# A graph-network layer in f32 on one core: Strassen's scheme for batch 0 as well, a first convolution group of 128 columns, and a new table of exchanged places

## The chip, the cores and the metric

The kernel runs on one core of a Trainium2 chip. Its time is the device time of one execution in microseconds; smaller is better. Three timed runs of the kernel before gave 2005.38, 2008.96 and 2012.02 us.

## The reference

For 32 graphs of 512 nodes with 256 features, everything in f32 (`x` is first normalised over its features and cut at 0; `h` is the result):

```python
xc = transpose(h, (0, 2, 1))
x_conv = relu(bn(conv1d(relu(bn(conv1d(xc, conv1_w, 0))), conv2_w, 8)) + xc)   # conv2 has 17 taps
s = h @ w_se.T + b_se                                  # 3 numbers for each node
A = exp(-(|s_n|^2 + |s_m|^2 - 2 s_n.s_m)) * adj        # 512 x 512 for each graph
x_nmp = A @ relu(h @ w_msg.T + b_msg)
gi = concat(x_conv, x_nmp) @ w_ih.T + b_ih             # three gates of 256: r, z, n
gh = h @ w_hh.T + b_hh
r, z = sigmoid(gi_r + gh_r), sigmoid(gi_z + gh_z)
n = tanh(gi_n + r * gh_n)
out = x + (1 - z) * n + z * h
```

## The kernel before

One function, `tile_adj_preln_gnn_kernel`, issues everything by hand. Its work is cut into five streams (`streams`), Python generators that each issue a small piece and then say when the next piece may go.

`rows` makes the first convolution (`conv1`, two 128x128 weights by 512 columns for each half of the output) of the batches that a group needs, and leaves it in `h1`. `begins` prepares the batches that come later: normalised input, transposed, stored to DRAM (`HD`), and read again by the users. `graphs` computes messages, the exponential (`kernel_exp`), the mask product (`masked`, on VectorE) and the gather (`gather`). `conv` is the second convolution, and `gates` the three gates of each batch (`gates(b)`, with one `unit(o)` for each half of the output features).

The second convolution is of Winograd's kind, nested twice. The 32 x 512 positions become 928 columns (29 for each batch, `U`), and these are cut into seven groups by `STARTS`. Each group has 25 products. VectorE prepares their operands (`operands`, `fives`, `ends`: the tiles `x` and `xd`), with weights `w` that are made in the first group and read back from DRAM (`wd`) in the others. A product of the first group is 16 matmuls (8 for one with a zero factor), as wide as the group; in the other groups a third operand makes 12 do. ScalarE takes the results out of PSUM (`n`, `z`), VectorE sums them (`summed`), and `evacuate` hands them to the batches.

The batches of a group are `batches(g)`, which counts those that have any column in it; a batch that straddles two groups is computed in both, with its own part of the columns. With the first boundary at 116 = 4 x 29 columns, the first group has exactly batches 0 to 3, and `G = 4` says so.

A gate batch is computed in a plain form or in Strassen's form, by one line:

```python
fast = FIRST_FAST <= b < B - PLAIN          # FIRST_FAST = 1, PLAIN = 1, B = 32
```

The plain form takes 18 matmuls of 512 columns for each half. The fast one treats the gates r and z as a 2 x 2 block product with seven products, each of 3 matmuls of 256 columns, and 6 of 512 columns for the third gate. It needs sums of the weights (`weight_sums`, once, in `wsum`) and of the data (`data_sums`, for each batch, in `t`). In it a PSUM bank is partly filled by ScalarE before TensorE adds to it:

```python
ps_z = acc.tile([P, N], F32, name="ps_acc")
act.activation(ps_z[:, lo], ps_r[:, lo], AF.Copy)
```

The order in which the streams are served is settled when the program is built. A planner keeps a model of each engine, computes when each stream can go on, and takes among the able streams the one whose clock is furthest behind. `OTHERS` is a table of exceptions: at the numbered choice it takes another one. While nothing is able, `keep_warm` issues dummy transposes of the identity (`ps_acc<-ident`), in the early part only. The batches up to 7 (`TURNED`) are transposed on TensorE, the later ones on VectorE.

Of the kernel before, what the change touches and what calls it, by code (L numbers as in the profile page):

```python
# [31 lines left out]
G = 4  # L32
U = 29
Q = 18

STARTS = (0, 116, 252, 388, 523, 658, 793, 928)
NG = len(STARTS) - 1
UG = max(j - i for i, j in zip(STARTS, STARTS[1:]))
PER = (STARTS[-1] - STARTS[1]) / (NG - 1) / U
TURNED = 8  # L40
# [10 lines left out]
def kernel(  # L51
# [32 lines left out]
    B, N, D = x.shape  # L84
# [4 lines left out]
    def sizes(g):  # L89


        nu = STARTS[g + 1] - STARTS[g]
        return nu, ND * nu, 2 * ND * nu, ND * (nu + 1)
# [98 lines left out]
    def elements(t):  # L192
        n = 1
        for k in t.shape[1:]:
            n *= k
        return n
# [52 lines left out]
    def on_pe(out, ins, took):  # L249
        nonlocal now  # L250
        now = max(now, after("PE", [out], ins)) + took
        note("PE", [out], ins, now + 0.163)

    def matmul(ps, lhsT, rhs, **more):
        nonlocal narrow
        few = lhsT.shape[0] < 32
        on_pe(ps, [lhsT, rhs], (0.2675 if few else max(0.2145, 0.005 + elements(ps) / 600.0)) + 0.1 * (few != narrow))
        narrow = few
        nc.tensor.matmul(ps, lhsT, rhs, **more)  # L259
# [88 lines left out]
    def load_gates(b):  # L348
        if b >= B or b in HB:
            return  # L350
        settle_stores()
        HB[b] = late.tile([P, ND, N], F32, name="hTb", bufs=2)
        sp.dma_start(HB[b], HD[b])
        HB_AT[b] = done(HB[b])
# [21 lines left out]
    def load_sums(b):  # L376
        if b < B and b not in XN:
            settle_stores()
            XN[b] = late.tile([P, ND, N], F32, name="xnb", bufs=2)
            for d in range(ND):  # L380
                sp.dma_start(XN[b][:, d, :], ND_[b, d])
            XN_AT[b] = done(XN[b])
# [17 lines left out]
    ident = const.tile([P, P], F32, name="ident")  # L400
# [27 lines left out]
    def input_of(g):  # L428
        return h1[:, : Q * sizes(g)[3]].rearrange("p (q i v) -> p q i v", q=Q, i=ND)

    def zeros(g):
        at = input_of(g)
        for b in range(B + 1):
            v = U * b - STARTS[g]
            if 0 <= v <= sizes(g)[0]:
# [94 lines left out]
    def conv1(g, b, o):  # L530

        hT = HT[b] if g == 0 else HR[b]
        v0, at = U * b - STARTS[g], input_of(g)
        first, last = max(0, -v0), min(U, sizes(g)[0] - v0)
# [178 lines left out]

    RING = 6
    PLAIN = 1
    FIRST_FAST = 1
    W_BASE, taken = [], 0

    def new_w():
# [178 lines left out]
    def batches(g):  # L898

        return range(STARTS[g] // U, (STARTS[g + 1] - 1) // U + 1)  # L900
# [195 lines left out]
    def weight_sums():  # L1096


        for k, w in enumerate((whh, wih[:, :ND], wih[:, ND:])):
            a11, a12 = w[:, 0, :D], w[:, 1, :D]  # L1100
            a21, a22 = w[:, 0, D : 2 * D], w[:, 1, D : 2 * D]
            s1, s2, s4 = (wsum[:, k, j, :] for j in range(3))
            dve.tensor_tensor(s1, a21, a22, op=ALU.add)
            dve.tensor_tensor(s2, s1, a11, op=ALU.subtract)
            dve.tensor_tensor(s4, a12, s2, op=ALU.subtract)
            dve.tensor_tensor(a21, a11, a21, op=ALU.subtract)

    OPEN, NEW, NEW_DONE, NEW_B, MIXED = 0, [], [], [FIRST_FAST], [0, 0]
    UPDATED, LEFT = [0, 0], [0]
    T_AT, T_STEP = {}, {}  # L1110
    sums_free = [FIRST_FAST, FIRST_FAST]

# [120 lines left out]
    def begin(b):  # L1233

        nonlocal begun, turning
        if b >= TURNED:
            yield lambda: b not in NORMS
            yield NORM_AT[b]  # L1240
            xs = XS.pop(b)
            pool.dma_start(XD_[b].rearrange("(c p) d -> p c d", p=P), xs)
            yield done(XD_[b])
            xb = xs.rearrange("p c d -> p (c d)").rearrange("p (o n) -> p o n", o=ND)
            for o in range(ND):
                blocks(xb[:, o, :], XD_[b].rearrange("(k i) d -> i k d", i=32), o)
            yield max(done(xb), front.free("hT", 2))
            settle_stores()
            HT[b] = front.tile([P, ND, N], F32, name="hT", bufs=2)
            turning = True  # L1250
            for o in range(ND):
                dve.transpose(HT[b][:, o, :], xb[:, o, :])
                if o < ND - 1:
                    yield dve.free
            yield dve.free + 0.4
            pool.dma_start(HD[b], HT[b])
            begun, turning = b + 1, False
            if b + 1 < B:
                later(now + 0.3, lambda: load(b + 1))
            return  # L1260
        if b == 2:
            yield lambda: told > 0
        yield lambda: b not in NORMS
        yield NORM_AT[b]
        turning = True
        for d in range(ND):
            yield gps.free("ps_g")
            norm_t(b, d)
            if d == ND - 1:
                begun, turning = b + 1, False  # L1270
                if b < 2 or G <= b < TURNED - 1:
                    load(b + (G if b < 2 else 2))
            yield now

    def rows(g, b):
        nonlocal made, made_at
        for o in range(ND):
            yield gps.free("ps_g")
            conv1(g, b, o)
            if o == ND - 1 and b == batches(g)[-1]:  # L1280
                made, made_at = g + 1, act.free + LAG
            yield now
        HT.pop(b, None)
# [43 lines left out]
    def gates(b):  # L1327
# [11 lines left out]
        hT = HB[b]  # L1339
# [77 lines left out]

        fast = FIRST_FAST <= b < B - PLAIN
        if b == B - PLAIN:
# [24 lines left out]
        def unit(o):  # L1444
# [55 lines left out]
            if fast:  # L1500
                if o == 0:
                    if b == FIRST_FAST:
                        weight_sums()
# [10 lines left out]
                def term(ps, weight, data, begin=False, end=False, of=(0, 1, 2)):  # L1514
                    for k in of:
                        w, t = sources[k]
                        matmul(
                            ps, weight(k, w), data(k, t),
                            start=(begin and k == 0), stop=(end and k == 2), skip_group_check=True,
                        )  # L1520

                def given(i, g):
                    return lambda k, w: w[:, i, cols(o, g)]
# [4 lines left out]
                def part_of(i, s):  # L1528
                    return lambda k, t: t[:, i, s]
# [25 lines left out]
                    yield XN_AT[b]  # L1555
                term(ps_r[:, lo], given(0, 0), part_of(0, lo), of=(2,))
                ps_z = acc.tile([P, N], F32, name="ps_acc")
                act.activation(ps_z[:, lo], ps_r[:, lo], AF.Copy)
                copy_at = act.free + LAG
                yield now  # L1560
# [48 lines left out]
                if o == 0:  # L1609
                    load_gates(b + 1)  # L1610
                    if b == FIRST_FAST:
                        load_sums(b + 1)
# [17 lines left out]
            if not fast:  # L1630
# [15 lines left out]
                else:  # L1646
                    parts = []
                    for s in (slice(0, N - P), slice(N - P, N)):
                        ps = acc.tile([P, N], F32, name="ps_acc")
                        parts.append((ps, s))  # L1650
                        for i in range(ND):
                            matmul(
                                ps[:, s], whh[:, i, cols(o, 2)], hT[:, i, s],
                                start=(i == 0), stop=(i == ND - 1), skip_group_check=True,
# [4 lines left out]
                ps_z = acc.tile([P, N], F32, name="ps_acc")  # L1659
# [13 lines left out]
            for ps, s in parts:  # L1673
                for j in range(2 * ND):
                    matmul(
                        ps[:, s], wih[:, j, cols(o, 2)], x_in[j][:, s],
                        start=False, stop=(j == 2 * ND - 1), skip_group_check=True,
# [5 lines left out]
        for o in range(ND):  # L1683
            yield from unit(o)
# [56 lines left out]
            yield from graph(b)  # L1741

    def all_begins():
        for b in range(G, B):
            yield lambda: b in XS and not rows_wait
            yield from begin(b)

# [1 line left out]

    def all_rows():  # L1750
        nonlocal rows_wait
        for b in range(G):
            yield from begin(b)
            yield act.free + LAG
            yield from rows(0, b)
        for g in range(1, NG):
            for b in batches(g):
                yield lambda: (
                    freed >= g - 1 and begun > b and not turning and at_product >= 25 * g - 4
                )  # L1760
                if b == batches(g)[0]:
                    zeros(g)
                rows_wait = True
                yield front.free("hT", 2) - 0.5
                load_row(b)
                if b + 1 in batches(g) and b + 1 < begun:
                    later(max(now + 2.5, front.free("hT", 2) - 0.5), lambda b=b: load_row(b + 1))
                yield HR_AT[b]
                yield from rows(g, b)
                del HR[b]  # L1770
                rows_wait = b + 1 in HR

    def all_gates():
# [17 lines left out]


    OTHERS = {
        6: 1, 41: 1, 259: 1, 374: 1, 430: 1, 443: 1, 547: 1, 953: 1, 979: 1, 1020: 2,
        1022: 1, 1182: 1, 1202: 1, 1260: 1, 1291: 1, 1471: 1, 1636: 1, 1670: 1, 1744: 1,
        1745: 1, 1837: 1, 2031: 1, 2149: 1, 2232: 1, 2391: 1, 2604: 1, 2610: 1,
    }
    choices = 0
    unused, waits = acc.tile([P, N], F32, name="ps_acc"), 0
# [113 lines left out]
```

## Time and profile before

| what | value |
|---|---|
| median of three timed runs | 2008.96 us |
| the profiled execution, its own time | 2015.27 us |
| its span, first to last instruction | 2013.5 us |
| mean granted TensorE clock | 0.991 |
| PE busy | 1973.8 us, 98% |
| DVE busy | 1505.0 us, 75% |
| ACT busy | 874.1 us, 43% |
| POOL busy | 478.5 us, 24% |

PE is TensorE, DVE VectorE, ACT ScalarE, POOL GpSimd, and SP the engine that only issues DMAs here. In the rows of the profile an operation is written as output<-inputs by the names of tiles; nearly all have the line of a helper, so they are told apart by tiles: `ps_c` are the products of the second convolution, `ps_acc` the gates (and the dummies), `ps_g` all else. An f32 matmul leaves two records. What stands in brackets behind a row is the idle time before it and what ended it.

### The profile page before, as it was taken

To read this page: it belongs to the slowest core of one execution; us is meant where nothing else is said; L and a number is where in the kernel's file an instruction comes from. 1 tells how busy PE (TensorE), PEld (TensorE's weight loads), DVE (VectorE), ACT (ScalarE), POOL (GpSimd) and SP (SyncE) were. 2 spreads that over 40 slices of the span, in tenths; PEclk is the share of its full clock that TensorE was granted. 3 is DMA by queue.
4 is the path that set the end of the run, shared out by engine and by line. 5 is a ranking of instruction groups with operands and counts; after the bars stand their busy time and mean duration, and the time that the engine had idled before them with its cause. 6 is when DMAs were issued, how large, how long until landed. Compare 5 with 4: busy or idle time off the path is not lost.

```text
span 2013.5 us, 28526 instructions
## 1 busy us (share of the span) xinstructions
PE 1973.8 (98%) x9692; PEld 1450.8 (72%) x9692; DVE 1505.0 (75%) x2711; ACT 874.1 (43%) x1755; POOL 478.5 (24%) x628
## 2 busy tenths in 40 slices
PE   8999999999999999999999999999999999999998
PEld 5887666776778677776787776777776777776774
DVE  6889589976988597876787775688894877766443
ACT  6644463434634455333464235463334453324321
POOL 3222112222212132222231221232220221113232
PEclk9999899999999999999999999999999999999999
DMA  8446777888898788889787886798895876665564
GB/s 295 168 174 211 238 241 194 211 209 197 227 252 208 194 191 213 200 195 222 146 235 192 204 202 162 191 246 203 179 211 150 185 171 155 157 151 106 111 100 34
DMA packets 578177, 378.92 MB, mean 188 GB/s; under 512 B 457664, under 2 KB 475488, under 8 KB 576896
## 3 DMA queue, kind: packets, MB, share of 16 engines
q1 hardware_dynamic: 419760, 279.15, 49.7%
q0 software_dynamic: 157184, 97.81, 26.4%
q8 instruction: 77, 1.26, 0.2%
q14 instruction: 68, 0.56, 0.1%
q10 hardware_dynamic: 1088, 0.13, 0.0%
HBM read 278.94 MB, written 114.56 MB: 195 GB/s over the span
## 4 chain that ended last, share of the span: by engine, by line
PE 65%; DVE 4%; issue 2%; DMA 1%; ACT 1%; POOL 1%; DVEq 0%; POOLq 0%; SPq 0%; ACTq 0%
PE ps_acc L259 36%; PE ps_c L259 16%; PE ps_g L259 13%; DVE o_sb L241 1%; DMA cd<-part 1%; PE ps_g L265 1%; DVE t L241 0%; POOL out_dram L228 0%; DVE x L241 0%; DMA hd<-hT 0%; POOL cd L228 0%; DVE ps_acc L241 0%; ACT at L241 0%; DVE z L241 0%; DMA w<-wd 0%
## 5 line engine op out<-in xcount | busy, mean ns | idle before, releaser
L228 POOL DMA_DIRECT2D out_dram<-o_sb x252 | 275.8, 1719 | 636.5 <-DVE o_sb L241 510.9
L259 PEld LDWEIGHTS ps_c<-xd,w 128*128 128x128 f32 x2304 | 285.5, 190 | 49.9 <-ACT ps_c L241 33.9
L259 PEld LDWEIGHTS ps_c<-x,w 128*128 128x128 f32 x2032 | 259.8, 194 | 48.2 <-issue 32.9
L259 PE MATMUL ps_c<-xd,w 128*128 128x135 f32 (+1 forms) x2304 | 290.4, 279 | 3.9 <-ACT ps_c L241 3.9
L259 PE MATMUL ps_c<-x,w 128*128 128x135 f32 (+2 forms) x2032 | 268.5, 281 | 2.8 <-DVE x L241 2.8
L259 PE MATMUL ps_g<-at,msg 128*128 128x512 f32 x512 | 230.0, 600 | 3.5 <-DVE at L241 3.5
L241 DVE TENSOR_TENSOR ps_acc<-ps_acc,r 128x256 f32<-128x256 f32 x120 | 51.7, 431 | 230.4 <-PE ps_acc L259 209.3
L259 PE MATMUL ps_acc<-hTb,whh 128*128 128x512 f32 (+2 forms) x532 | 211.4, 495 | 1.4 <-ACT r L241 1.4
L259 PE MATMUL ps_acc<-xconv,wih 128*128 128x512 f32 (+2 forms) x532 | 211.6, 495 | 0.7 <-DVE ps_acc L241 0.7
L259 PE MATMUL ps_acc<-xnb,wih 128*128 128x512 f32 (+2 forms) x532 | 209.1, 496 | 3.2 <-DVE ps_acc L241 3.2
L259 PEld LDWEIGHTS ps_g<-at,msg 128*128 128x128 f32 x512 | 96.9, 193 | 112.8 <-issue 103.4
L259 PE MATMUL ps_acc<-t,wsum 128*128 128x256 f32 x720 | 175.7, 380 | 1.2 <-DVE wsum L241 1.2
L259 PEld LDWEIGHTS ps_acc<-t,wsum 128*128 128x128 f32 x720 | 135.7, 191 | 35.5 <-issue 17.9
L259 PEld LDWEIGHTS ps_acc<-xconv,wih 128*128 128x128 f32 x532 | 98.0, 190 | 48.3 <-issue 38.6
L259 PE MATMUL ps_g<-hT,w 128*128 128x512 f32 (+8 forms) x296 | 124.5, 571 | 7.4 <-DMA hT<-hd 6.8
L259 PEld LDWEIGHTS ps_acc<-xnb,wih 128*128 128x128 f32 x532 | 96.1, 190 | 44.8 <-issue 31.5
L259 PE MATMUL ps_g<-wmsg,hTg 128*128 128x259 f32 x496 | 124.4, 382 | 0.0
L259 PE MATMUL ps_acc<-t,wih 128*128 128x256 f32 x480 | 123.2, 380 | 0.0
L259 PEld LDWEIGHTS ps_acc<-hTb,whh 128*128 128x128 f32 x532 | 94.7, 190 | 38.5 <-issue 28.3
L241 DVE TENSOR_TENSOR x<-x 128x544 f32<-128x544 f32 (+2 forms) x175 | 120.2, 707 | 0.3
L241 ACT ACTIVATE ps_c<-ps_c 128x270 f32<-128x270 f32 (+1 forms) x144 | 56.3, 391 | 137.9 <-PE ps_c L259 137.7
L241 ACT ACTIVATE h<-ps_g,bn_shift,bn_scale 128x252 f32<-128x252 f32 (+8 forms) x212 | 86.3, 484 | 60.4 <-PE ps_g L259 60.4
(157 smaller groups left out, 3251.3 us busy)
## 6 DMA issues: line engine op xcount, KB each, us to landing
w<-wd SPq DMA_DIRECT2D x414, 256.0 KB, 4.0
m_sb<-in_adj_dram SPq DMA_DIRECT2D x384, 64.0 KB, 3.4
wd<-w POOLq DMA_DIRECT2D x74, 256.0 KB, 3.3
hT<-hd SPq DMA_DIRECT2D x33, 512.0 KB, 4.0
hd<-hT POOLq DMA_DIRECT2D x32, 512.0 KB, 6.1
hTb<-hd SPq DMA_DIRECT2D x32, 512.0 KB, 4.6
xnb<-nd SPq DMA_DIRECT2D x64, 256.0 KB, 3.3
out_dram<-o_sb POOLq DMA_DIRECT2D x252, 64.0 KB, 4.8
```

The lines of the kernel that those rows point to most:

```text
L228: self.engine.dma_start(dst, src, **more)
L241: getattr(self.engine, op)(*tiles, **more)
L259: nc.tensor.matmul(ps, lhsT, rhs, **more)
L265: nc.tensor.transpose(ps, a, ident)
```

## The change

Four things change together. `STARTS` gives the first group 128 columns and the others 134, 134, 133, 133, 133, 133 (before: 116, and then 136, 136, 135, 135, 135, 135). Batch 4 so lies in the first group with 12 of its 29 columns and in the second with the rest; the loops that counted to `G` now count by `batches(0)`. `FIRST_FAST = 0` puts batch 0 into Strassen's form, with the sums of the weights made ahead of it. One matmul with the identity is issued into the first `ps_z` bank, ahead of the activation that overwrites half of it. And `OTHERS` has 60 entries instead of 27.

```diff
-STARTS = (0, 116, 252, 388, 523, 658, 793, 928)
+STARTS = (0, 128, 262, 396, 529, 662, 795, 928)
...
     PLAIN = 1
-    FIRST_FAST = 1
+    FIRST_FAST = 0
...
                 ps_z = acc.tile([P, N], F32, name="ps_acc")
+                if b == 0 and o == 0:
+                    matmul(ps_z, ident, hT[:, 0, :], start=True, stop=True)
                 act.activation(ps_z[:, lo], ps_r[:, lo], AF.Copy)
...
     def all_begins():
-        for b in range(G, B):
+        for b in range(batches(0)[-1] + 1, B):
...
     def all_rows():
         nonlocal rows_wait
-        for b in range(G):
+        for b in batches(0):
             yield from begin(b)
             yield act.free + LAG
             yield from rows(0, b)
...
     OTHERS = {
-        6: 1, 41: 1, 259: 1, 374: 1, 430: 1, 443: 1, 547: 1, 953: 1, 979: 1, 1020: 2,
...
+        107: 1, 115: 1, 134: 2, 184: 1, 186: 1, 251: 1, 329: 1, 343: 2, 385: 1, 497: 1,
...
```

## The prediction

> **What bounds the kernel now.** I read the core's span first, then the shares of busy time:
>
> ```profile
> core 0: 2013.5 us, clock 0.991
> ```
>
> ```profile
> PE 1973.8 (98%) x9692; PEld 1450.8 (72%) x9692; DVE 1505.0 (75%) x2711; ACT 874.1 (43%) x1755; POOL 478.5 (24%) x628
> ```
>
> TensorE is busy for 98% of the span, so the end is set by the sum of its matmuls and by its few stalls (2013.5 - 1973.8 = 39.7 us idle, some 6 of them behind the last matmul). A group's mean duration is a matmul's latency, and matmuls overlap; what a matmul costs is the distance from start to start. So the timeline of PE came next (start, us, operation, count; an f32 matmul leaves two records, so x16 are 8 matmuls):
>
> ```profile
> 60.35 1.94 PE L259 MATMUL ps_c<-x,w 128*128 128x116 f32 x16
> 62.12 0.60 PE L265 MATMUL ps_g<-ident,m_sb 128*128 128x128 f32 x4
> ...
> 1605.98 1.88 PE L259 MATMUL ps_acc<-xconv,wih 128*128 128x512 f32 x4
> 1607.70 1.08 PE L259 MATMUL ps_c<-x,w 128*128 128x135 f32 x8
> 1608.62 1.46 PE L259 MATMUL ps_acc<-t,wsum 128*128 128x256 f32 x6
> 1609.91 0.60 PE L259 MATMUL ps_acc<-hTb,whh 128*128 128x256 f32 x2
> ...
> 2006.12 0.61 PE L259 MATMUL ps_acc<-xconv,wih 128*128 128x128 f32 x4
> 2006.57 0.61 PE L259 MATMUL ps_acc<-xnb,wih 128*128 128x128 f32 x4
> ```
>
> One matmul: 116 columns (62.12 - 60.35) / 8 = 0.221 us (0.2225 is the median of such stretches), 135 columns 0.92 / 4 = 0.230, 256 columns 1.29 / 3 = 0.430, 512 columns 1.72 / 2 = 0.860, 128 columns 0.45 / 2 = 0.225. Between 135 and 512 columns a column costs 0.63 / 377 = 1.67 ns. At that slope 116 columns would take 0.198; they take 0.2225. So narrow matmuls sit on a floor, and the first group's 116 columns are paid like some 130.
>
> The last view is where TensorE stalls early on, with what released it in brackets, and the mean granted clock beside it (fifth engine column, then PEclk):
>
> ```profile
> 53.90 0.69 PE L259 MATMUL ps_acc<-right,left 5*128 5x512 f32 x1 [1.35 <-ACT right L241]
> ...
> 55.53 3.67 PE L259 MATMUL ps_c<-x,w 128*128 128x116 f32 x16 [0.49 <-DVE x L241]
> ...
> 177.70 7.04 PE L259 MATMUL ps_g<-at,msg 128*128 128x512 f32 x16
> ...
> 201.76 5.37 PE L259 MATMUL ps_g<-hT,w 128*128 128x512 f32 x8 [2.94 <-DMA hT<-hd]
> ...
> 237.15 10.20 PE L259 MATMUL ps_g<-at,msg 128*128 128x512 f32 x16 [2.36 <-DVE at L241]
> ```
>
> ```profile
> 150.00:200.00 50.00, 46.52 (x314) 38.25 (x312) 48.12 (x86) 23.83 (x60) 13.07 (x31) 1.00 0.68 204
> 200.00:250.00 50.00, 45.29 (x193) 28.65 (x194) 27.81 (x51) 22.03 (x51) 6.14 (x10) 0.86 0.72 243
> ```
>
> The same 16 records take 7.04 us at 177.7 and 10.20 behind a stall at 237. VectorE is 96% busy from 150 to 200 us.
>
> **The change part by part.**
>
> *Columns of the convolution.* A group after the first runs 12 matmuls for each of 24 products and 8 for the one with a zero factor: 296, and 6 x 296 = 1776 in all. Each loses 2 columns: 1776 x 2 x 1.67 ns = -5.9 us. If the floor already bends the line between 116 and 135 columns (7.5 ns / 19 = 0.4 ns a column), it is -1.4. I take the upper slope, since 136 columns (0.2325) against 135 show no flattening. The first group's 392 matmuls grow from 116 to 128 columns; the row of that width is 0.225, so 392 x 2.5 ns = +1.0 (0 if both lie on the floor). Sum -4.9, between -0.4 and -5.9.
>
> *Strassen for batch 0.* Plain: each half is 18 matmuls of 512 columns. In seven products: 21 of 256 and 6 of 512. Two halves remove 24 x 0.860 = 20.6 us and add 42 x 0.430 = 18.1, and the clearing product is one more at 0.860: -1.7 us. VectorE gets 13 more operations (4 adds of 256 columns at 0.43 us, 3 sums of 512 at 0.68 and 6 of 256 at 0.42: 6.3 us) and ScalarE 4 copies of 256; both lie beside the 18 us of these products and the convolution between them, and without that cover TensorE would wait for the sums. The clearing product stands ahead of the copy that fills half of its bank, so this copy and what ScalarE has behind it come 0.86 us later once; ScalarE is 43% busy and takes that up. The sums of weights (12 adds at 0.42 us = 5.0 us of VectorE) move from batch 1 to batch 0, so from about 345 us, where TensorE waited 1.2 us for them, to about 250 us.
>
> *Rows, moved steps and dummies.* Batch 4's preparation moves into the stream of the first group's rows. Its issues are the same, the load of batch 6's input on SP and the store of its transposed rows on POOL, only earlier; SP has 1302 issues before and after, POOL 631 instead of 630 instructions, and neither queue shows TensorE waiting for it before 197 us, so 0. Batch 4 is split, 40 first-layer matmuls replace 36 at 72 columns more in all: +0.1 us. There are 8 more dummy transposes of 0.11 us, +0.9; they stand where the schedule expects TensorE to wait.
>
> *The start.* The first product now needs five batches instead of four. In the built order, between the second exponential's products (end at 55.1 us) and the second gather, TensorE has batch 4's and half of batch 5's transposes, 4 mask transposes, batch 4's first layer and 5 dummies: 0.9 + 0.9 + 1.8 + 1.5 + 0.6 = 5.7 us. The gather waits for the fourth mask product, and on VectorE this is queued behind the two instructions that start the operands, of 1548 columns together, which wait for batch 4's activations. I put these at 60.5: 55.1, 1.8 of transposes, 0.8 until ScalarE has emptied their bank, 1.5 of first layer, and 1.3 for its last activations. Then 60.5 + 1.9 + 0.7 = 63.1. So the gap is 63.1 - 55.1 - 5.7 = 2.3 us, plus some low clock afterwards, against 0.49 before and a 1.7 us slow first product. I take +2.5 with the small waits further on; bounds -1 and +8 (a microsecond for each dummy).
>
> *The switch to the second group.* Before, TensorE lost 2.94 us for a DMA of rows, and 2.36 for the fourth mask. Behind them it ran slow: 5.37 - 3.60 = 1.8 and 10.20 - 7.04 = 3.2, and 1.8 more in between (218.7 to 224.8), 12.1 in all. The Trainium skill ("TensorE: Matmul & The Clock Gate", part 1 on the clock gate) says that the clock halves after an idle window of about 3.4 us; by that rule stalls under 3 us would cost only themselves, 5.3 us. The trace speaks otherwise (0.86 granted over that window), and I follow it: a stall of over 2 us is paid about twice. In the new order 7.1 us of other work lies between the first two blocks of rows instead of 2.7, and 2.8 us more (the second group's first product) between the last two mask transposes and the gather. So the second stall should go with its slow gather (-5.6), and half of the first is doubtful. The sums of weights, which VectorE does in one piece with about nine operations queued behind them, may bring 1 to 2 us. I take -4.5, between -12 and +3; by the rule it would be about -2.
>
> *VectorE in the first group.* Its operands are 516 wide instead of 468: 45 operations x 0.05 = 2.3 us, the wide ones 1.4, the sums behind the products 2.9; 6.6 us more before 235 us, and about as much less in all later groups together. TensorE's own time per product hardly grows. I take +1; bounds 0 and +7.
>
> *The new table* changes the order of hundreds of later pieces; the tail after the last product of the convolution is instruction for instruction the same for the last 40 us. In the middle of the trace stalls and slow stretches sum to some 30 us, each decided by a neighbour; I take 0, plus or minus 6.
>
> Sum: -4.9 - 1.7 + 0.1 + 0.9 + 2.5 - 4.5 + 1.0 = -6.6 us. The profiled execution took 2015.27 (its span 2013.5 and 1.8 around it), above all three timed runs, so the difference is taken from their median: 2008.96 - 6.6, rounded 2002.5.
>
> **The rivals.** *The gain goes back in stalls.* The start costs 6 to 8 instead of 2.5 and the switch keeps its first stall: -6.6 + 4.5 + 2.3 = 0, about 2008.5. For it: the order was settled by planned durations, not by the low clock behind a stall. Against: the rows are visibly better covered. That the narrower products save only 1.4 us (the floor) leads to about 2007, in the same place.
>
> *Slower: VectorE bounds the first group.* Place: the products from 70 to 235 us. It is 96% busy from 150 to 200, and TensorE already waited 0.56 and 1.75 us there for x. If it has no slack from the late start on, its 6.6 us all land on TensorE, in some four stalls of over 1.5 us that each bring about 1.7 us of low clock, and the late start costs its 8: -6.6 - 1 - 2.5 + 6.6 + 6.8 + 8 = +11, about 2020; with half of the stalls 2016. It decides once VectorE is over about 97% busy from 100 to 200 (before: 91.5 of 100 us).
>
> **How the numbers follow.** Forecast 2002.5: 0.55 (own range 1994 to 2008). Given back: 0.24 at 2008. VectorE-bound: 0.21 at 2017. What a measurement of this kernel can tell from no change is about 0.3%, 6 us. Faster by more: 0.37 from the first case (the part of its range below 2003, where most of the doubt about the switch lies) and 0.04 from the second; same: 0.18 + 0.18 + 0.02; slower: 0.02 + 0.19. The range 1992 to 2014 leaves out the better half of the switch and order bounds and the worst of the third case.
>
> **What would show it.** Right: PE busy about 1967 us, 392 matmuls of 128 columns at 0.225 and those of 133 at 0.227 start to start, one ident product into ps_acc, the wait before the second gather near 2 us, no wait of over 1.5 us with low clock between 195 and 250. Wrong: 133 columns at 0.230 (no gain of columns); waits of ps_c for DVE x of over 4 us in all before 240; idle of over 45 us in all; new waits for wsum of over 2 us.

## The result, and the profile after

Five timed runs of the changed kernel gave a median of 2022.46 us (2019.06 to 2026.61), five of the kernel before, measured beside them, 2012.02. The medians are 10.4 us apart; the ratio of the comparison is 1.0076 (15 us), with a 95% interval of 1.0057 to 1.0094, which is 11 to 19 us. So the changed kernel is slower, where 6.6 us less was forecast. The profiled execution of the changed kernel took 2025.84 us; its span is 10.6 us longer than that of before. The core's span and the shares of busy time:

```profile
core 0: 2024.1 us, clock 0.990
```

```profile
PE 1971.6 (97%) x9746; PEld 1454.8 (72%) x9746; DVE 1506.0 (74%) x2724; ACT 873.0 (43%) x1765; POOL 478.0 (24%) x629
```

TensorE's busy time fell by 2.2 us; its idle time rose from 39.7 to 2024.1 - 1971.6 = 52.5. So TensorE did not get more to do, it stood still more often. The timeline of PE gives the cost of one matmul again, from start to start:

```profile
79.07 3.73 PE L259 MATMUL ps_c<-x,w 128*128 128x128 f32 x32
82.64 0.60 PE L265 MATMUL ps_g<-ident,x_sb 128*128 128x128 f32 x4
...
777.76 1.98 PE L259 MATMUL ps_c<-x,w 128*128 128x133 f32 x16
779.58 0.59 PE L259 MATMUL ps_acc<-t,whh 128*128 128x256 f32 x2
```

128 columns: (82.64 - 79.07) / 16 = 0.223 us; 133 columns: (779.58 - 777.76) / 8 = 0.2275. Over the whole trace the medians are 0.2232, 0.2275 and 0.230 for 128, 133 and 134 columns, against 0.2225, 0.230 and 0.2325 for 116, 135 and 136 before. The narrower products pay what the prediction said. What was lost stands in the stretches (us, then busy time of PE, PEld, DVE, ACT and POOL, granted clock, share of the DMA engines, GB/s). First the kernel before, in two stretches not shown so far:

```profile
50.00:100.00 50.00, 48.16 (x340) 40.88 (x339) 40.51 (x86) 32.36 (x71) 10.82 (x17) 0.97 0.50 172
...
250.00:300.00 50.00, 50.00 (x269) 35.65 (x268) 41.54 (x79) 30.96 (x54) 9.24 (x15) 1.00 0.76 244
```

And the changed kernel:

```profile
50.00:100.00 50.00, 43.05 (x255) 34.09 (x254) 31.88 (x74) 23.74 (x54) 7.58 (x12) 0.90 0.37 128
...
150.00:200.00 50.00, 47.22 (x290) 37.11 (x290) 49.24 (x78) 19.55 (x47) 11.50 (x20) 0.97 0.59 182
200.00:250.00 50.00, 47.14 (x279) 35.48 (x278) 36.71 (x65) 28.16 (x72) 8.17 (x23) 1.00 0.66 220
250.00:300.00 50.00, 45.36 (x223) 34.15 (x222) 42.00 (x82) 26.77 (x48) 9.90 (x17) 0.93 0.79 258
```

The stretch from 200 to 250 us became good (clock 1.00 instead of 0.86). The one from 50 to 100 lost 5.1 us of busy PE and 0.07 of clock, and the one from 250 to 300, faultless before, lost 4.6 us and 0.07.

To add this up I went through the timeline of PE row by row. The distance from a row's start to the next is split into three: its matmuls at the costs above, the wait in brackets, and the rest. Waits plus rest by stretch are called the loss here. The rest is low clock in part only: the mean granted clock (0.991 before, 0.990 after) allows about 18 us of it in the whole span of before and about 21 in the changed kernel. What is left, 25 to 31 us of it from 400 us on in all the kernels here, is small distances between unlike matmuls and missing records. So the differences between losses can be read, to a few us; their sizes alone cannot. A few missing records leave some 2 us of doubt in the first of the three.

| stretch, us | loss before | loss after | difference |
|---|---|---|---|
| to 56 | 17.0 | 16.9 | 0 |
| 56 to 110 (start) | 1.1 | 9.7 | +8.6 |
| 110 to 240 (first group, first rows of the second) | 18.9 | 9.7 | -9.2 |
| 240 to 300 (switch, batch 0's gates) | 0.1 | 9.4 | +9.3 |
| 300 to 400 | 4.4 | 2.1 | -2.3 |
| from 400 on | 46.1 | 54.0 | +7.9 |
| the matmuls themselves | | | -3.5 |

The sum is +10.8, the difference of the spans +10.6. From 400 us on the difference is mostly waits: up to the last matmuls TensorE was idle for 16.1 us before and for 21.7 after, and the low clock lasted 13.7 us in both.

*The start.* The timeline of PE in the changed kernel:

```profile
54.58 0.69 PE L259 MATMUL ps_acc<-right,left 5*128 5x512 f32 x1 [1.25 <-ACT right L241]
...
57.50 1.97 PE L265 MATMUL ps_g<-ident,x_sb 128*128 128x128 f32 x8 [1.41 <-ACT at L241]
59.26 1.06 PE L265 MATMUL ps_g<-ident,m_sb 128*128 128x128 f32 x4
...
66.06 0.27 PE L272 MATMUL ps_acc<-ident 128*128 128x128 f32 x1
70.63 8.60 PE L259 MATMUL ps_g<-at,msg 128*128 128x512 f32 x16 [4.29 <-DVE at L241]
```

Two waits of over a microsecond, then transposes at half speed (1.06 us where 0.60 is usual), and the second gather behind a wait of 4.29 us (and then in 8.60 us, where the same 16 records took 7.04 before). VectorE's own timeline tells what the fourth mask product (`at<-ps_g,at`) was queued behind:

```profile
60.42 0.69 DVE L241 TENSOR_TENSOR at<-ps_g,at 128x512 f32<-128x512 f32 x1 [7.47 <-ACT hT L241]
64.52 0.69 DVE L241 TENSOR_TENSOR at<-ps_g,at 128x512 f32<-128x512 f32 x1 [3.41 <-PE ps_g L265]
65.12 0.42 DVE L241 BATCH_NORM_STATS2 st<-x_sb 128x6 f32<-128x256 f32 x1
...
67.38 0.17 DVE L241 TENSOR_SCALAR veps<-mv 128x4 f32<-128x4 f32 x1
67.45 0.68 DVE L241 TENSOR_TENSOR at<-ps_g,at 128x512 f32<-128x512 f32 x1
68.06 1.83 DVE L241 TENSOR_TENSOR x<-h 128x1290 f32<-128x1290 f32 x2
69.80 0.68 DVE L241 TENSOR_TENSOR at<-ps_g,at 128x512 f32<-128x512 f32 x1
```

Between the second mask product and the third stand nine instructions of batch 6's statistics (65.12 to 67.45), between the third and the fourth the two wide starters of the operands. The idle time in front (7.47 and 3.41 us) shows that VectorE had no other work ready then.

*The switch.* Around batch 0's gates, the timeline of PE and then that of VectorE:

```profile
267.16 0.69 PE L259 MATMUL ps_c<-right,left 5*128 5x512 f32 x1 [1.71 <-ACT right L241]
...
270.07 2.16 PE L259 MATMUL ps_c<-x,w 128*128 128x134 f32 x8 [1.76 <-DVE w L241]
272.02 1.06 PE L265 MATMUL ps_g<-ident,m_sb 128*128 128x128 f32 x4
272.87 3.08 PE L259 MATMUL ps_c<-xd,w 128*128 128x134 f32 x16
```

```profile
264.56 0.42 DVE L241 TENSOR_TENSOR wsum<-whh 128x256 f32<-128x256 f32 x1
...
268.99 0.42 DVE L241 TENSOR_TENSOR wih<-wih 128x256 f32<-128x256 f32 x1
269.33 0.68 DVE L241 TENSOR_TENSOR w<-w 128x512 f32<-128x512 f32 x1
```

Twelve sums of weights in one piece, and behind them the third operand's `w`, for which the convolution waited. The product at 270.07 took 1.95 us to the next start, where 8 records of 134 columns take 0.92.

### The profile page after: what moved, and what is told of

Read it like the earlier page. It is cut to its first block, busy times and chain, and to the rows that moved or that the text cites. A ratio compares the mean times of both kernels' runs of the same rounds, so it can differ in the third digit from the quotient of the medians.

```text
span 2024.1 us, 28623 instructions
## 1 busy us (share of the span) xinstructions
PE 1971.6 (97%) x9746; PEld 1454.8 (72%) x9746; DVE 1506.0 (74%) x2724; ACT 873.0 (43%) x1765; POOL 478.0 (24%) x629
## 4 chain that ended last, share of the span: by engine, by line
PE 64%; DVE 5%; issue 4%; DMA 3%; POOL 2%; ACT 2%; SPq 0%; DVEq 0%; POOLq 0%; ACTq 0%
PE ps_acc L259 35%; PE ps_c L259 16%; PE ps_g L259 13%; DVE o_sb L241 1%; DMA cd<-part 1%; DMA hT<-hd 1%; POOL cd L228 1%; POOL out_dram L228 1%; DVE x L241 1%; DVE t L241 1%; SPq L228 0%; DVE ps_acc L241 0%; PE ps_g L265 0%; DMA hd<-hT 0%; DVE at L241 0%
## 5 line engine op out<-in xcount | busy, mean ns | idle before, releaser
L259 PEld LDWEIGHTS ps_c<-xd,w 128*128 128x128 f32 x2304 | 283.5, 190 | 46.1 <-ACT ps_c L241 34.9
L259 PE MATMUL ps_c<-xd,w 128*128 128x133 f32 (+1 forms) x2304 | 289.2, 278 | 3.8 <-ACT ps_c L241 3.4
L259 PE MATMUL ps_c<-x,w 128*128 128x133 f32 (+2 forms) x2032 | 266.5, 280 | 5.3 <-DVE w L241 3.4
L259 PE MATMUL ps_acc<-xconv,wih 128*128 128x256 f32 (+2 forms) x524 | 207.5, 492 | 1.5 <-DVE ps_acc L241 1.3
L259 PE MATMUL ps_acc<-xnb,wih 128*128 128x256 f32 (+2 forms) x524 | 206.1, 491 | 1.5 <-DVE ps_acc L241 1.5
L259 PE MATMUL ps_acc<-t,wsum 128*128 128x256 f32 x744 | 180.8, 379 | 0.0
L259 PEld LDWEIGHTS ps_acc<-t,wsum 128*128 128x128 f32 x744 | 139.9, 190 | 35.8 <-issue 19.4
L259 PE MATMUL ps_acc<-t,wih 128*128 128x256 f32 x496 | 128.5, 382 | 0.0
L259 PE MATMUL ps_g<-hT,w 128*128 128x512 f32 (+10 forms) x304 | 120.6, 544 | 5.4 <-DMA hT<-hd 4.0
L241 DVE TENSOR_TENSOR x<-x 128x536 f32<-128x536 f32 (+2 forms) x175 | 120.3, 707 | 0.2
L241 ACT ACTIVATE h<-ps_g,bn_shift,bn_scale 128x252 f32<-128x252 f32 (+12 forms) x216 | 88.0, 482 | 54.6 <-PE ps_g L259 54.3
L241 ACT ACTIVATE ps_c<-ps_c 128x266 f32<-128x266 f32 (+1 forms) x144 | 55.7, 387 | 127.9 <-PE ps_c L259 127.6
```

What stands on the lines that cost most here:

```text
L241: getattr(self.engine, op)(*tiles, **more)
```

## The experiments

Theory S says that the loss is stalls made by the order on VectorE and ScalarE, and the low clock behind them. Its rivals were that VectorE as a whole limits the first group, and that the parts of the change cost what they cost whatever the order. The expectations below name their theories for themselves: a letter means what that text says of it.

**The parts without a table.** The table of either kernel is numbered for its own sequence of choices, so a part alone was compared with the table emptied (`OTHERS = {}`). All four kernels then follow the planner's plain rule.

```diff
# before, no table                # before with Strassen for batch 0, no table
-    OTHERS = {6: 1, 41: 1, ...}  -    FIRST_FAST = 1
+    OTHERS = {}                  +    FIRST_FAST = 0      (and the clearing product)
# the changed kernel without Strassen for batch 0, no table
-    FIRST_FAST = 0   (and without the clearing product)
+    FIRST_FAST = 1
```

Before, no table:

> The kernel before with the table of exchanged places empty. Theory S (the late start of the convolution costs what was lost): the old table is worth some us on the chip, this run 2012 to 2022, and the start to 110 us stays as in before (wait plus low clock about 18 us). Theory T (the new table is what lost the time): the old table was worth 10 us or more, 2022 or more, and the kernel after without a table is no slower than this.

Before with Strassen for batch 0, no table:

> Strassen for batch 0 and the clearing product alone (old column groups, no table). Both theories: 1 to 3 us under the before kernel without a table, since the matmuls shrink by 1.7 us; if the sums of weights at the switch to the second group cost (a third theory W), 2 to 5 us over it, with waits of ps_acc for wsum or t near 250 us.

The changed kernel without Strassen for batch 0 (so the columns alone), no table:

> The new column groups alone (first group 128 columns, batch 0 in the plain form, no table). Theory S: the start to 110 us loses 6 to 10 us more than in the before kernel without a table, the matmuls gain 4, sum +2 to +6. Theory T: start about +2, sum -2 to -5.

The changed kernel, no table:

> The kernel after with an empty table. Theory S: the sum of the two parts, 0 to +5 us against the before kernel without a table, and the new table is worth about as much as the old one was. Theory T: 4 to 7 us under the before kernel without a table, and the kernel after with its table (2022) is slower than this.

Measured: 2056.53, 2038.15, 2032.28 and 2031.46 us, in ratios to before 1.0254 [1.0236, 1.0272], 1.0158 [1.0138, 1.0178], 1.0129 [1.0112, 1.0146] and 1.0123 [1.0094, 1.0153]. Without a table the changed kernel is 25 us faster than before, with the tables 10 to 15 slower. The table was worth 49 us to before (2056.53 against 2007.73 on the same chip), and only 9 to the changed kernel. Of the four expectations one theory's range was met, T's for before without a table; the other three kernels came out 18 to 25 us under it, where no theory had put them.

**Is 25 us the worth of the change?** Three more orders that nobody chose, and the changed kernel with the table of before:

```diff
-    LAG = 0.17
+    LAG = 0.18      # before and the changed kernel, no table; before also with 0.16
```

> Before without its table, and with the planner's lag between an engine's result and its use at 0.18 us instead of 0.17: the same instructions in another order that nobody chose. Theory T (without a fitted table an order's stalls are drawn at random, so the times of kernels without a table say little of the change's parts): 2030 to 2070, at least 5 us from the 2056.5 of before without its table. Rival (the time without a table belongs to the program: the first group's 128 columns and Strassen's scheme for batch 0 each save 18 to 24 us): within 5 us of 2056.5.

> Before without its table, and with the planner's lag at 0.16 us instead of 0.17. Theory T: 2030 to 2070, and with the other kernel of this kind a spread of 10 us or more. Rival: within 5 us of 2056.5.

> The changed kernel without its table, and with the planner's lag at 0.18 us instead of 0.17. Theory T: 2020 to 2050, at least 5 us from the 2031.5 of the changed kernel without its table. Rival: within 5 us of 2031.5, and at least 15 below both kernels of before without a table.

> The kernel after with the table of the kernel before. Theory T (a table of exchanges belongs to one program; on another one it is an arbitrary order): 2025 to 2045, about as without a table (2031). Rival (the entries mend places that both programs share): 2000 to 2010.

Measured: 2055.82 and 2034.06 us for before, 2028.99 for the changed kernel, 2052.08 with the other's table, each from two runs. Neither theory held cleanly: with 0.18 both kernels stayed within 3 us, as the rival said; with 0.16 before came out 22 us lower, in theory T's range. And a table that gains 49 us on its own kernel costs the other one 21, more than either side had expected. The loss by stretch (one trace of each) says where the time depends on the order:

| kernel | 56-110 | 110-240 | 240-300 | 300-400 | from 400 |
|---|---|---|---|---|---|
| before, its table | 1.1 | 18.9 | 0.1 | 4.4 | 46.1 |
| before, no table | 2.2 | 16.5 | -0.2 | 9.5 | 80.0 |
| before, no table, 0.18 | 0.5 | 19.4 | 0.1 | 9.7 | 78.8 |
| before, no table, 0.16 | 1.1 | 19.0 | -0.3 | 9.4 | 65.2 |
| with Strassen alone, no table | 0.5 | 14.0 | 10.1 | 5.2 | 69.5 |
| with the columns alone, no table | 9.3 | 9.6 | 3.2 | 11.1 | 54.2 |
| changed, no table | 9.9 | 9.6 | 9.4 | 2.7 | 59.2 |
| changed, no table, 0.18 | 9.7 | 10.3 | 7.7 | 3.7 | 52.2 |
| changed, the table of before | 10.4 | 8.7 | 8.8 | 2.2 | 79.7 |
| changed, its table | 9.7 | 9.7 | 9.4 | 2.1 | 54.0 |

The first four columns belong to the parts: each kernel with the first group of 128 columns loses 9 to 10 us at the start, and 6 to 11 less than before up to 240 us; each one with Strassen for batch 0 loses 8 to 10 us at the switch, of which 4 to 8 come back before 400 in the kernels without a table, since the sums of weights are then done (where they are not done earlier, as in before without a table, TensorE waits 2.56 us for `w` at 350 us, behind the same twelve sums). The last column depends on the order: 52 to 80 us without a fitted table or with the wrong one. Whether the new columns have a share in it too was not separated: without a table the three orders with them lost 52 to 59, the four with the old columns 65 to 80, but with the table of before the new ones lost 80. The table of before had brought it down to 46; the new one leaves it at 54, where the changed kernel lies without any. So the changed kernel lacks 8 us of fit that before had.

**The masks first.** In the changed kernel 12 instructions are issued behind the fourth mask product instead of ahead of it: the nine of batch 6's statistics with their POOL operation, and the two starters. A counter in `Engine.issue` holds the named instructions back; the planner goes on as if nothing had moved, so the rest of the order is the same (the code is shortened here).

```diff
-    getattr(self.engine, op)(*tiles, **more)
+    put = lambda: getattr(self.engine, op)(*tiles, **more)
+    k = (self.name, COUNT.get(self.name, 0)); COUNT[self.name] = k[1] + 1
+    if k in HOLD: HELD.setdefault(HOLD[k], []).append(put)
+    else: put()
+    for f in HELD.pop(k, []): f()
# HOLD: DVE 113 to 121, POOL 23, DVE 123 and 124, all behind DVE 125
```

> The kernel after with 12 instructions moved and nothing else: at the start, batch 6's statistics (9 on VectorE, 1 on POOL) and the two wide instructions that begin the operands are issued behind the fourth mask product instead of ahead of it. Theory S (the first group's operands and statistics stand ahead of the masks, and this makes the 4.29 us wait before the second gather): the wait falls to about 1 us and low clock behind it goes, 4 to 6 us less in all, 2017 to 2019. Rival (the fifth batch's chain through transposes, ScalarE and first layer makes the wait, whatever VectorE does): the wait moves to the first product of the convolution, 0 to 1 us less.

Measured: 2016.9 us, ratio to before 1.0046 [1.003, 1.0061], so 6 us less than the changed kernel by the ratios, 5.6 by the medians. VectorE and then PE in this kernel:

```profile
63.88 0.69 DVE L245 TENSOR_TENSOR at<-ps_g,at 128x512 f32<-128x512 f32 x1 [3.02 <-PE ps_g L277]
64.97 1.35 DVE L245 TENSOR_TENSOR at<-ps_g,at 128x512 f32<-128x512 f32 x2 [0.40 <-PE ps_g L277]
66.24 0.42 DVE L245 BATCH_NORM_STATS2 st<-x_sb 128x6 f32<-128x256 f32 x1
```

```profile
66.47 7.10 PE L271 MATMUL ps_g<-at,msg 128*128 128x512 f32 x16 [0.77 <-DVE at L245]
```

The gather starts 4.2 us earlier. The queue on VectorE was the wait. Of the start's 9.7 us of loss 5.2 stay: 1.0 of waits, some 2.7 of low clock (most rows from 57 to 63 us took twice their time), and small distances.

**The sums of weights later.** The twelve sums are issued behind the `w` of the third operand instead of ahead of it.

```diff
# HOLD: DVE 419 to 430, behind DVE 431
```

> The kernel after with one move: the 12 sums of weights are issued behind the third operand w of the next product instead of ahead of it. Theory W (the sums, 4.9 us in one piece on VectorE, keep TensorE from that product at 270 us): the wait of 1.76 us there goes, with about 2 us of low clock behind it, 2 to 4 us less. Rival (the switch is bound by other work): the wait reappears within 10 us, no difference.

Measured: 2020.04 us (2012.16 to 2022.63), ratio 1.0053 [1.0036, 1.007]. The timeline of PE:

```profile
267.54 1.18 PE L269 MATMUL ps_c<-x,w 128*128 128x134 f32 x8
268.76 0.66 PE L275 MATMUL ps_g<-ident,m_sb 128*128 128x128 f32 x4
```

The wait of 1.76 us and the slow product are gone, and nothing waits for `wsum`. The loss from 240 to 300 fell from 9.4 to 5.7. The time fell by 2.4 us in the medians and 4.6 by the ratios, but the interval overlaps that of the changed kernel (1.0057 to 1.0094), so the trace shows this move, the time alone does not. The rest of the switch is the second exponential's `right` (1.50 us here) and what follows it.

**One mask ahead, in the kernel before.** The wait that the prediction wanted removed, removed without the rest of the change: the fourth mask product at 235 us is put ahead of three instructions of the convolution.

```diff
# in before; HOLD: DVE 385 to 387, behind DVE 388
```

> The kernel before with one move: at 235 us the fourth mask product goes ahead of three VectorE instructions of the convolution. Theory C (a stall over 2 us is paid about twice through the clock): the wait of 2.36 us falls to about 0.9, the gather behind it takes about 7 instead of 10.2 us, 3 to 5 us less. Rival (by the skill's rule the low clock does not come from this stall): only the 1.5 us of waiting go.

Measured: 2005.71 us, ratio 0.9989 [0.9978, 1.0].

```profile
236.65 7.13 PE L269 MATMUL ps_g<-at,msg 128*128 128x512 f32 x16 [0.78 <-DVE at L243]
...
245.50 1.20 PE L269 MATMUL ps_c<-x,w 128*128 128x136 f32 x8 [0.84 <-DVE w L243]
```

The wait went from 2.36 to 0.78 us, and with it the gather from 10.20 to 7.13: 1.58 of waiting brought 3.07 of low clock. A new wait of 0.84 for `w` behind it kept a part, and 3.0 of the 4.6 reached the median. By the ratio it is 2.2, with an interval that ends at 1.0: the low clock that went is read from the trace.

**Four moves together.** To the two moves above come two at large later stalls of the changed kernel. At 785 us an add into `ps_acc`, for which TensorE waited 2.76 us, goes ahead of the last three of five wide `x`. At 1066 us the copies `left` and `right`, for which it waited 3.05, go ahead of two `part` activations and their store; the first of these had ScalarE waiting 5.04 us for a DMA. Both stalls in the changed kernel:

```profile
785.97 0.70 PE L259 MATMUL ps_acc<-t,whh 128*128 128x256 f32 x2 [2.76 <-DVE ps_acc L241]
...
1069.71 0.69 PE L259 MATMUL ps_c<-right,left 5*128 5x512 f32 x1 [3.05 <-ACT right L241]
```

```diff
# also HOLD: DVE 1179 to 1181 behind DVE 1182;
#            ACT 1035, ACT 1039 and one DMA of POOL behind ACT 1041
```

> The changed kernel with four places of its order altered, all other instructions where they were: the 12 instructions in front of the fourth mask product of the second gather behind it (as in the run with the masks first), the 12 sums of weights behind the w of the third operand (as in the run with the sums later), the add into ps_acc near 785 us ahead of the last three of five wide x, and the two copies of ScalarE (left, right) near 1066 us ahead of two gate activations that wait for a DMA behind stores. Theory S (stalls of the order, and the low clock behind each, are the loss): the start gives 6, the switch 4, the add at 785 its 2.8 and some 2 of low clock, the copy at 1068 its 3.0 and some 2; less what the next neighbour takes, so 2006 to 2010, level with before. Rival (what is taken from one stall comes back in the next one): the two moves known give at most 8 together and the two others nothing, 2014 or more.

Measured: 2007.38 us (14 runs), ratio 1.0 [0.9992, 1.0008], against 1.0076 for the changed kernel. Theory S's number was met, the rival's was not. The profile of this kernel, its span and its largest waits of PE (total, times, longest):

```profile
core 0: 2005.9 us, clock 0.995
```

```profile
PE ps_acc L280 <- DVE ps_acc L254: 4.5, 8, 1.4
PE ps_g L280 <- DMA hT<-hd: 3.6, 2, 3.3
PE ps_g L280 <- DVE at L254: 2.8, 4, 1.1
```

The waits for `at` fell from 6.4 to 2.8 us, those for `right` ahead of `ps_c` from 4.8 to 1.7. The loss from 400 us on is 45.3, the level of before. So a change of order alone, four moves of 29 instructions and one store, takes away the difference between the changed kernel and before. Stalls remain, and with them the 3.5 us that the matmuls had gained. None of the kernels run is shown to beat before; nearest to it is before with its mask ahead, whose interval ends at 1.0.

**The low clock of the start.** Two waits of 1.24 and 1.41 us stand ahead of the low clock at 55 to 66 us. They were filled with dummy transposes, and in before the one of 1.35.

```diff
     def keep_warm(n):
         ...
+        CALLS.append(n)
+        for _ in range(MORE.get(len(CALLS), 0)):
+            nc.tensor.transpose(unused[:, :P], ident, ident)
# the changed kernel with the four moves: MORE = {13: 9, 15: 10}; before with its mask ahead: {12: 10}
```

> The changed kernel with its four moves, and 19 more dummy transposes (0.11 us each at full clock): 9 in the wait of 1.24 us before the second exponential's products at 54 us, 10 in that of 1.41 us before batch 4's transposes at 57 us. Theory W (the low clock of 0.58 and 0.73 between 55 and 65 us is what idle TensorE leaves behind it): the clock stays near 1 there, the 4 us of low clock go, and the time falls from 2007.4 to about 2003.5 to 2005. Rival (the clock there depends on the work, or the dummies come late and push the products away): the clock stays at 0.6 to 0.75 and the time at 2007 to 2009.

> The kernel before with its fourth mask moved ahead, and 10 more dummy transposes in the wait of 1.35 us before the second exponential's products at 54 us. Theory W: the first product of the convolution at 55.5 us takes 1.94 us instead of 3.67, and the time falls from 2005.7 by 2 to 3 us. Rival: the product stays at 3.67, and the time at 2005 to 2007.

Measured: 2010.69 us, ratio 1.0018 [1.0009, 1.0026], and 2005.35, ratio 0.9995 [0.9983, 1.0006]. First the stretch in the kernel with four moves, then the same with the dummies:

```profile
55.00:60.00 5.00, 3.59 (x20) 3.21 (x17) 0.10 (x1) 4.85 (x10) 0.00 (x0) 0.58 0.00 0
60.00:65.00 5.00, 5.00 (x26) 4.13 (x25) 1.29 (x3) 2.76 (x6) 0.60 (x1) 0.73 0.75 265
```

```profile
55.00:60.00 5.00, 3.88 (x34) 2.77 (x27) 0.69 (x1) 5.00 (x11) 0.00 (x0) 1.00 0.09 10
60.00:65.00 5.00, 4.35 (x31) 3.75 (x29) 2.06 (x4) 2.96 (x7) 1.13 (x2) 1.00 0.83 269
```

The mechanism is as theory W had it: with the waits filled the clock stays at 1.00. The time is not: the first of the two lies above the range of either theory. A part goes into a new wait of 0.80 us for ScalarE's `hT`, which the slow transposes had hidden, so the gather starts only 1.36 us earlier (65.12). That lead still stands at 223 us, and is lost there, behind a wait of 1.32 us that both kernels have. With the four moves alone, and then with the dummies too:

```profile
225.11 0.66 PE L286 MATMUL ps_g<-ident,augr 128*128 128x128 f32 x4 [1.32 <-ACT h L254]
225.60 3.74 PE L280 MATMUL ps_c<-x,w 128*128 128x128 f32 x32
```

```profile
223.71 0.65 PE L286 MATMUL ps_g<-ident,augr 128*128 128x128 f32 x4 [1.32 <-ACT h L254]
224.21 5.36 PE L280 MATMUL ps_c<-x,w 128*128 128x128 f32 x32
```

The same work behind the same wait takes 3.74 us in one and 5.36 in the other, at a clock of 1.00 and of 0.50 from 225 to 228 us. Cut where the clock can change, with the four moves alone and then with the dummies too:

```profile
223.11:226.52 3.41, 2.09 (x19) 1.90 (x19) 0.93 (x1) 3.33 (x12) 1.12 (x2) 1.00 0.77 266
226.52:229.94 3.42, 3.42 (x34) 2.94 (x32) 3.39 (x6) 1.59 (x5) 1.83 (x3) 1.00 0.55 171
...
221.19:224.60 3.41, 2.09 (x20) 1.90 (x19) 0.40 (x1) 3.33 (x12) 1.12 (x2) 1.00 0.71 226
224.60:228.02 3.42, 3.42 (x18) 3.42 (x18) 3.42 (x5) 2.11 (x6) 1.84 (x3) 0.50 0.51 159
```

TensorE was busy for the same 2.09 us in the piece with the stall, and the next piece was granted 1.00 in one kernel and 0.50 in the other. What decides between them is open. In before the first product became shorter (2.51 instead of 3.67 us), but the low clock came after it instead, and the median didn't move. That the changed kernel with dummies is 3 us slower than without in the median is not explained by this; its profiled span is 1.5 us longer, and which of the later stalls makes the rest is open.

## Why the prediction was wrong

Forecast -6.6, happened +10.4 on the medians and +10.6 on the spans, which the steps are set against. Three steps failed: the start, the switch (its term for the sums of weights) and the table. Of the 17.2 us between forecast and spans 6.1 lie at the start, 4.6 at the switch and 7.9 past 400 us; 2.1 are matmuls that saved less, 2.3 came back from 300 to 400 us, and the 1.0 taken for VectorE was not needed. The steps, by their names there:

- *Columns of the convolution* (-4.9) held. Each of the 1776 matmuls of the later groups saves 2.5 ns, each of the 392 of the first costs 0.7 more: -4.2. *Strassen for batch 0* as matmuls (-1.7) rests on the costs of 256 and 512 columns, 0.43 and 0.86 again; all matmuls together came to -3.5 with 2 us of doubt, against -5.6 forecast with the dummies.
- *The start* (+2.5, up to 8) failed: +8.6, with a wait of 4.29 us where 2.3 was worked out. The place was right, the size was not. The step counted two instructions ahead of the fourth mask on VectorE and overlooked nine more ahead of the third; moving both took about 6 us away. It also had TensorE done at 60.8 us, at full speed. TensorE was done at 66.3, because of the wait of 1.41 us for the exponential's `at`, which the step did not contain, and half-speed transposes. And with the first product moved back, nothing covered this: VectorE was busy for 4.7 of the 5 us from 55 to 60 before, and for 0.0 after.
- *The switch* (-4.5) came to about 0. The half that was worked out was right and even too small: 110 to 240 us gained 9.2 of the 12.1 that it had named as lost there, and the mask experiment shows the mechanism, a stall of 2.36 us paid with 3.07 more. The half that was waved through was wrong: "may bring 1 to 2 us" for the sums of weights was 9.3 in the stretch, 2.3 of it returned before 400. The prediction saw the nine operations queued behind them but named no one who waits for these; it was the convolution, for `w`. Moving the sums took 3.7 us of this stretch's loss. Its stated parts (-5.6, -2.3 by the rival's account, +1 to 2) also sum to about -6.4, not to the -4.5 that it took. In the kernels without a table Strassen's part adds 6 to 10 here.
- *The new table* (0, plus or minus 6) failed as an argument. It took the middle of the trace for noise of equal size on both sides. But before had been fitted: of the 65 to 80 us that its instructions lose past 400 us without a table, its own left 46. The new table starts from the changed kernel's own 52 to 59, and left 54. Past 400 us that cost 7.9 us.
- *VectorE in the first group* (+1) held, and with it the rival "VectorE bounds the first group" fell, though the measured time lies near its number. VectorE was 49.24 of 50 us busy from 150 to 200, beyond the rival's 97% for this half, and from 100 to 200 it was 93.8%. All waits of `ps_c` for VectorE's `x` sum to 0.3 us. An engine at 98% was not the bound there, because the operands that it prepares were ahead of TensorE.
- *The gain goes back in stalls* was the right rival, and stopped too early: it had the start at its upper bound but the switch's second stall removed at no price, and no price for the table.
- Of the *signs* that it gave for being wrong one came, idle time of over 45 us (52.5). It had looked for a new wait for `wsum`; the one that came was for `w`.

On the clock, the choice against the Trainium skill's figure ("TensorE: Matmul & The Clock Gate", part 1, a clock that halves after an idle window of about 3.4 us) was right: a stall of 2.36 us, and two of 1.24 and 1.41, were followed by low clock, and with them shortened or filled it went. But the same section also says that the window runs free, so that what happens depends on where in it the work falls. The traces agree in part: after the first 30 us their low clock comes in pieces of 3.41 us or a multiple, as long as the window that the section speaks of. But the 1.32 us stall, which cost nothing in one kernel and 1.6 us in the other, lay in one such piece in both, so no run here shows what decided there. The "about twice" of the prediction is no rule either: with the low clock behind it the stall of 2.36 us cost 2.3 times its length, that of 4.29 us at the start 1.4 times (its gather took 8.60 us instead of 7.04).

## What to carry to other kernels

When work is moved, list every instruction that stands ahead of the awaited one on each in-order engine, in the built order, and start the sum from where the engine is when it really arrives, waits and low clock included; an estimate that counts only the instructions named in the diff is a lower bound. An order that was fitted to a kernel is part of its time: a change that alters the sequence has to win back the fit before its own gain is seen, so compare the parts without the fit, stretch by stretch, and repair the few largest stalls of the new order before judging the change. A busy share of 98% on a supporting engine says nothing until someone waits for it.

## What the runs showed of the hardware

The granted clock was 1.00 or 0.50, nothing between, and in the sixteen traces every stretch of low clock inside the span lasted 3.41 us, 6.83 or, once, 10.24. A stretch of 3.41 us at 0.50 holds back 1.7 us of work at most, whatever the length of the stall ahead of it. If the spans are cut at these places from 30 us on, all 60 pieces in which TensorE was idle for more than 2.0 us were followed by one at 0.50, and 32 of the 63 with 1.5 to 2.0 us; below that it was 25 of 122 with 1.0 to 1.5 us and 27 of some 4360 with less.

So a stall's price was not a fixed multiple of its length. Behind 2.36 us the following gather of 16 records took 10.20 us, behind 0.78 us 7.13; behind 1.24 and 1.41 us the clock was 0.58 from 55 to 60 us, and 1.00 with the stalls filled by transposes of the identity; behind 1.32 us it was 1.00 in one kernel and 0.50 in another with the same instructions there. A fill therefore pays only where the low clock, and not the engine next in line, is what ends the stretch: here it removed some 2.5 us of low clock and moved the gather by 1.36.
